# Low part of a block's products by TensorE in some blocks, and list and row products moved to other steps

## The chip, the cores and the metric

The kernel runs on one core of one Trainium2 chip. The metric is the device time of one execution in microseconds (us). Before the change it is 1099.06 us, the median of three runs (1097.8 to 1101.74). Profiles come from one further execution.

The engines are named as in the profile: PE is TensorE (PEld its weight loads), DVE is VectorE, ACT is ScalarE, POOL is GpSimd, and SP issues most of the DMAs.

## The reference

One layer of an edge-gated graph network: 16 graphs of 1024 nodes with 256 features, one sparse weighted adjacency for all of them.

```python
pre_u = jnp.einsum('bud,dk->buk', h_t, W1[:d])
pre_v = jnp.einsum('bvd,dk->bvk', h_t, W1[d:])
hidden = jax.nn.relu(pre_u[:, :, None, :] + pre_v[:, None, :, :] + b1)
S = jax.nn.sigmoid(jnp.einsum('buvk,ko->buvo', hidden, W2)[..., 0] + b2[0])
a_t = jnp.einsum('buv,bud->bvd', S * A_a, h_t)
m_t = jnp.einsum('uv,bud->bvd', A_m, h_t) * h_t
z_t = beta1 * h_t + beta2 * (jnp.einsum('bvd,de->bve', a_t, Wa) + ba) \
    + beta3 * (jnp.einsum('bvd,de->bve', m_t, Wm) + bm)
```

Here `A_a` and `A_m` are both the adjacency. Most of it is zero, so the kernel computes gates only for the edges that are there: it fetches the rows of the neighbours u of a node v.

## The kernel before

**Blocks and steps.** The 16 graphs form 4 groups of 4; the 1024 nodes v form 8 tiles of 128. A block is one group with one tile: 32 blocks, numbered k, in the order of `order` (groups 0 and 1 interleaved in blocks 0 to 15, group 2 in 16 to 23, group 3 in 24 to 31). A block has 10 steps (two windows of 64 nodes, five steps each), so there are 320 steps; n numbers them and s = n mod 10 is the step in its block. In a step 128 edges are handled for the four graphs of the group: the row `fetched` holds, for the edge's node u, four pre-activations and four feature rows.

**One step.** POOL gathers `fetched` (L518) from a table in DRAM, up to 8 steps ahead. PE makes `pc`, the row of pre_v for each edge, as a product of a 0/1 matrix `mark` with `X` (L607, function `expand`, two steps ahead; there are two PSUM buffers named pc). DVE adds `pc` to `fetched` (L639, `add`, one step ahead), and then for each of the four graphs takes relu times W2 with a sum (L647, `gate`). ACT takes the sigmoid (L650) and multiplies the edge's weights with it into `left` (L652). PE sums the neighbours' rows with these weights into `acc` (L664, `aggregate`), two steps' worth in every second step.

**Once in a block.** `halves` makes `X` for the next block, that is pre_v with its bias. The product with `mark` rounds its operands to a shorter format (float32r), so X holds the high part of a value and the low part that the rounding left out: rows 0 to 63 of a window's X are one part of its 64 nodes and rows 64 to 127 the other. In the kernel before, ACT copies the product `p` out twice, as X in the short format (L482) and as `low` in full (L483); DVE subtracts the one from the other (L484); ACT copies both parts to the other half of the rows (L486, L489). Further, a block's end: `half_end` copies `acc` to `ev`, `turn_over` transposes it with `ident` (L682, copied by L685 into `LT`), `block_end` multiplies with Wa and Wm (L713), DVE adds beta1 h (L719) and SP stores.

**Rows and lists.** `rows` makes the table rows of pre_u by PE (L445 with w_u), in two halves with a copy by ACT each (L461), and SP writes them to the table; a row's x and hT are loaded some steps before. `plan` says at which step n each load and each half stands: `loads` and `at`. The products of 8 tiles of groups 0 and 1 are made in the first 51 steps, those of group 2 in steps 68 to 142, those of group 3 in 148 to 222. `lists` makes the lists of neighbours for a tile of nodes: tiles 0 to 3 ahead of the first step, tiles 4 to 7 between the steps, started at the steps of `start_list`. It is a generator: at `yield "op"` it gives way after one DVE operation, at "step" it asks for a later step for its PE work (L289, L341), at "load" and "wait" it pauses for some steps. `piece_of` turns these words into step numbers, and `fill` puts one piece between the operations of `gate`.

**What sets the order.** The order on each engine is written out by hand (a manual schedule): the loop over n issues everything, and each engine executes its own instructions in that order. In step n of the later part the order is: `gather_in` (aggregates and refetches), `add(n + 1)`, `gate(n)`, `left_adj(n + 1)`, `expand(n + 2)`, and then `products(n)`: row products, transposes, block end and the parts of `halves`. `after(step, f)` puts a piece at a later step.

**PSUM.** There are two buffers named `pc` and two named `misc`. The products `p` of `rows` and `halves`, the transposes `pt`, the block end `pz` and the list products `pl` all take turns in the two `misc` buffers, in the order in which they are issued. Who wants a buffer waits until the user before the last has been copied out.

Of the kernel before, what the change touches and what calls it, by code (L numbers as in the profile page):

```python
# [7 lines left out]
FP = mybir.dt.float32  # L8
FR = mybir.dt.float32r
I32 = mybir.dt.int32  # L10
AF = mybir.ActivationFunctionType
# [6 lines left out]
def kernel(  # L18
# [82 lines left out]
    def fixed(shape, name, dt=FP):  # L101
        return const.tile(shape, dt, name=name)
# [70 lines left out]
    slot_of = fixed([P, NW, TW], "slot_of")  # L173
    for w in range(NW):
        nc.vector.tensor_scalar(slot_of[:, w, :], upto[:, :TW], float(P), row, ALU.mult, ALU.add)
    ident = fixed([P, P], "ident")
    nc.vector.tensor_scalar(ident, upto[:, :P], row, None, ALU.is_equal)
    place = upto[:, :W].rearrange("p (q v) -> p q v", v=V)
    slot, nth = upto, upto[:, :S]

# [39 lines left out]
    def small(name):  # L220
        return psm.tile([P, 512], FP, name="misc")
# [20 lines left out]
    def lists(vt):  # L242
# [32 lines left out]
                nc.vector.scalar_tensor_tensor(keys, keys, top[:, s + 7:s + 8], keys, ALU.is_lt, ALU.mult)  # L275
                yield "op"

        used = lst.tile([P, S], FP, name="used", bufs=4)
        nc.vector.tensor_scalar(used, top, 0.0, None, ALU.is_gt, ALU.add, accum_out=R[:, 0:1])
        yield "op"  # L280
        nc.vector.tensor_scalar(R[:, 2:3], row, float(N), float(vt * P * N), ALU.mult, ALU.add)
# [6 lines left out]
        for i in range(4):  # L288
            nc.tensor.matmul(pw[:, i:i + 1], sums[:, i].rearrange("p w q v -> p (w q v)"), R[:, 0:1],  # L289
                             start=True, stop=True)  # L290
        yield "wait"
        first = R[:, 1:2]
        from_ = lst.tile([P, 1], FP, name="from", bufs=4)
# [176 lines left out]

    cuts = {}

    def halves(k):
        X = cuts[k] = big.tile([P, NW, GD], FR, name="X")
        low = one.tile([P, GD], FP, name="low")
        for h in range(2):
            step = yield
            c = slice(2 * h * D, (2 * h + 2) * D)
            p = small("p")
            add_row(p, b1_p)  # L480
            half_product(p, hTs[order[k]], w_v, h, True)
            nc.scalar.copy(X[:, 0, c], p)  # L482
            nc.scalar.copy(low[:, c], p)  # L483
        after(step + (2 if k else 1), lambda: nc.vector.tensor_tensor(low, low, X[:, 0, :].bitcast(FP), ALU.subtract))  # L484
        yield
        nc.scalar.copy(X[W:, 1, :], X[W:, 0, :].bitcast(FP))  # L486
        for w in range(NW):
            yield
            nc.scalar.copy(X[(1 - w) * W:(2 - w) * W, w, :], low[w * W:(w + 1) * W])  # L489
# [133 lines left out]
    def piece_of(r, n):  # L623

        said = next(r[0], None)
        if said is None:
            running.remove(r)
        else:
            r[1:] = said not in ("slot", "step"), n + {"load": 4, "wait": 2, "slot": 1, "step": 1}.get(said, 0)

    def fill(n, gap=True):
        for r in running:
# [3 lines left out]

    def add(n):
        t = fetched[at_slot[n]][:, :GD]
        nc.vector.tensor_tensor(t, t, pcs.pop(n), ALU.add)  # L639

    def gate(n):
        m = len(QUARTERS[n % TW])
# [120 lines left out]


    advance = {0: (3,), 2: (3,), 4: (3,)}
    start_list = dict(zip((0, 16, 48, 88), range(EARLY, NT)))
    loads, at = {}, {}

    def plan(blocks, ns):

        for k, (load, *pieces) in zip(blocks, ns):
            loads[load] = k
            at.update((n, k) for n in pieces)

    plan(turn[NT:], ((0, 1, 8), (1, 9, 12), (9, 18, 19), (13, 22, 28), (20, 29, 32), (29, 38, 39), (33, 42, 48), (40, 49, 51)))
    for g, first in ((2, 60), (3, 140)):
        plan([(g, vt) for vt in range(NT)], ((first - 4 + 10 * i, first + 8 + 10 * i, first + 12 + 10 * i)
                                             for i in range(NT)))
    plan([(1, vt) for vt in range(FIRST)], [(37 + 10 * i,) for i in range(FIRST)])
    plan([(g, vt) for g in range(2) for vt in range(FIRST, NT)], ((103,), (113,), (125,), (133,)))  # L780
# [19 lines left out]
    def products(n, k, s):  # L800
        nonlocal end, parts
        made_rows(n)
        if (s == 2 and 0 < k < BS) or n == total:
            turn_over(k - 1, 1, 1, n)
        z = 3 if n < ROOM else 4
        if z <= s < z + 4 and 0 < k < BS:
            if s == z:
                end = block_end(k - 1)
                next(end)
            go(end, n)  # L810
        if ROOM <= n < total - T:
            if s in (8, 9):
                turn_over(k, 0, s - 8, n)
        elif s == 7 and k < BS:
            turn_over(k, 0, 0, n)
        if s == 7 and k == BS - 1 or s == 8 and n < ROOM:
            turn_over(k, 0, 1, n)
        if (s == 0 and 0 < k < BS) or n == total - 1:
            turn_over(k - (s == 0), 1, 0, n)
        if n == total - 2:  # L820
            end = tail(tails[:2], n)
            next(end)
        elif n == total - 1:
            go(end, n)
        elif n >= total:
            end = tail([tails[2 + n - total]], n)
            next(end)
            go(end, n)
            go(end, n)
        later = n >= ROOM  # L830
        if k + 1 < BS and s - later in (0, 2, 3, 5, 6):
            if s == later:
                parts = halves(k + 1)
                next(parts)
            go(parts, n)

# [22 lines left out]
    done = 0  # L859
    for n in range(total + 2):  # L860
        k, s = divmod(n, T)
        if n < total - 3:
            last_in = n - 1 if n % 2 or n < ROOM else done
        else:
            last_in = n
# [170 lines left out]
```

## Time and profile before

| quantity | value |
|---|---|
| median of 3 runs | 1099.06 us |
| the profiled execution: its own time | 1101.12 us |
| its span, first to last instruction | 1099.3 us |
| busy PE, DVE | 1022.2 us (93%), 1025.4 us (93%) |
| busy ACT, POOL | 872.5 us (79%), 464.3 us (42%) |
| mean granted PE clock | 0.975 |
| DMA, mean over the span | 359 GB/s |

Busy time says how long an engine had an instruction in hand. The matmuls' ends are modelled and matmuls overlap, so a matmul's mean duration is longer than the distance from one to the next. PE and DVE are both busy 93% over the whole span; which of them sets the pace is to be read stage by stage. Blocks can be found in the trace by DVE's additions L639: every tenth begins a block. The first begins at 65.3 us, the last block ends at 1076.1.

### The profile page before, as it was taken

The numbers are of one execution on the slowest core, as the hardware profiler recorded it, in microseconds if no ns is written. First come the engines' busy times: TensorE is split into PE (matmuls) and PEld (weight loads), VectorE is DVE, ScalarE is ACT, GpSimd is POOL, SyncE is SP. The second block draws the span as 40 slices with busy tenths as digits, with TensorE's granted clock in tenths as the row PEclk, the third lists the DMA queues.
The fourth block names the chain that finished last, engine by engine and source line by source line (L and its number), as shares of the span: only waits on it lengthen the run. The fifth ranks groups of instructions, "written<-read, shape, count | busy, mean of one in ns | idle before, by whom it ended". The sixth has DMA issues, their size and how long they took to land.

```text
span 1099.3 us, 23917 instructions
## 1 busy us (share of the span) xinstructions
PE 1022.2 (93%) x7645; PEld 726.5 (66%) x7645; DVE 1025.4 (93%) x3487; ACT 872.5 (79%) x2616; POOL 464.3 (42%) x453
## 2 busy tenths in 40 slices
PE   7777889999899999999999999999999999999986
PEld 6654556776667666676777677767766666666653
DVE  8788888898999999999999999999999999999994
ACT  3347667787778888888988889888889888888873
POOL 2746575445347433563334343433343333333330
PEclk9988989999899999999999999999999999999999
DMA  9999799999999999999999999999999999999991
GB/s 285 331 391 311 295 327 303 356 394 382 384 343 344 391 410 381 384 378 396 408 382 400 406 400 398 386 398 388 353 362 383 372 350 357 359 372 363 354 335 42
DMA packets 149030, 394.54 MB, mean 359 GB/s; under 512 B 18224, under 2 KB 96048, under 8 KB 112688
## 3 DMA queue, kind: packets, MB, share of 16 engines
q0 software_dynamic: 50240, 300.11, 69.6%
q1 hardware_dynamic: 85360, 79.71, 22.9%
q10 hardware_dynamic: 13296, 13.11, 3.6%
q8 instruction: 62, 1.02, 0.3%
q14 instruction: 72, 0.59, 0.1%
HBM read 396.93 MB, written 50.33 MB: 407 GB/s over the span
## 4 chain that ended last, share of the span: by engine, by line
PE 39%; DVE 32%; issue 10%; ACT 9%; DMA 6%; POOL 2%; another core or an unknown queue 0%; SPq 0%; POOLq 0%; DVEq 0%; ACTq 0%
DVE fetched L647 15%; DVE fetched L639 12%; PE acc L664 10%; PE misc L713 10%; PE misc L445 7%; PE pc L607 7%; ACT left L652 3%; PE misc L682 2%; DMA hT<-in_xT_dram 2%; DMA hT<-in_x_dram 2%; PE misc L449 1%; DMA fetched<-table,uidx 1%; DVE low L484 1%; DVE h_blk L719 1%; DVE LT L696 1%
## 5 line engine op out<-in xcount | busy, mean ns | idle before, releaser
L518 POOL DMA_INDIRECT fetched<-table,uidx x320 | 345.5, 1080 | 540.9 <-PE acc L664 384.1
L647 DVE SCALAR_TENSOR_TENSOR fetched<-fetched,w_b 128x256 f32<-128x256 f32 x1280 | 476.5, 418 | 0.0
L639 DVE TENSOR_TENSOR fetched<-fetched,pc 128x1024 f32<-128x1024 f32 x320 | 387.9, 1212 | 38.1 <-PE pc L607 23.1
L652 ACT ACTIVATE left<-left,gt 128x32 f32<-128x32 f32 (+1 forms) x1280 | 299.5, 304 | 10.4
L664 PE MATMUL acc<-fetched,left 128*32 128x256 f32 x4096 | 271.7, 390 | 5.9 <-ACT left L652 4.6
L607 PE MATMUL pc<-X,mark 128*128 128x512 f32 x640 | 245.9, 466 | 12.1 <-DVE fetched L639 12.0
L664 PEld LDWEIGHTS acc<-fetched,left 128*32 128x32 f32 x4096 | 123.7, 111 | 113.1 <-issue 38.8
L650 ACT ACTIVATE gt<-sc,b_b 128x4 f32<-128x4 f32 x320 | 95.5, 298 | 94.8 <-DVE fetched L647 84.4
L607 PEld LDWEIGHTS pc<-X,mark 128*128 128x128 f32 x640 | 106.3, 191 | 91.8 <-issue 48.9
L713 PE MATMUL misc<-w_a,LT 128*128 128x256 f32 x496 | 118.7, 383 | 0.0
L713 PE MATMUL misc<-w_m,LT 128*128 128x256 f32 x496 | 117.2, 379 | 0.0
L445 PE MATMUL misc<-w_v,hT 128*128 128x256 f32 x448 | 108.1, 385 | 1.0 <-DMA hT<-in_xT_dram 1.0
L682 PE MATMUL misc<-ident,ev 128*128 128x128 f32 x512 | 81.3, 282 | 27.0 <-ACT low L483 9.3
L713 PEld LDWEIGHTS misc<-w_a,LT 128*128 128x128 f32 x496 | 94.7, 191 | 15.7 <-issue 0.4
L713 PEld LDWEIGHTS misc<-w_m,LT 128*128 128x128 f32 x496 | 93.9, 189 | 15.2
L617 ACT ACTIVATE left<-onehot,val 128x64 f32<-128x64 bf16 (+1 forms) x320 | 102.9, 322 | 0.0
L385 POOL DMA_INDIRECT val<-in_adjT_dram,vidx x80 | 87.6, 1095 | 33.2 <-issue 18.9
L647 DVE DVE_READ_ACCUMULATOR fetched<-fetched,w_b 128x1 f32 x1280 | 100.4, 78 | 0.0
L682 PEld LDWEIGHTS misc<-ident,ev 128*128 128x128 f32 x512 | 61.2, 143 | 55.1 <-ACT low L483 14.7
L445 PEld LDWEIGHTS misc<-w_v,hT 128*128 128x128 f32 x448 | 86.6, 194 | 16.0 <-DMA hT<-in_xT_dram 1.9
L672 ACT COPY ev<-acc 128x512 f32<-128x512 f32 x128 | 74.7, 584 | 15.4 <-PE acc L664 6.8
L685 ACT COPY LT<-misc 128x512 f32<-128x512 f32 x128 | 73.1, 572 | 5.6 <-PE misc L682 2.9
(178 smaller groups left out, 974.6 us busy)
## 6 DMA issues: line engine op xcount, KB each, us to landing
h_blk<-table SPq DMA_DIRECT2D x62, 256.0 KB
out_dram<-h_blk SPq DMA_DIRECT2D x62, 256.0 KB
hT<-in_xT_dram SPq DMA_DIRECT2D x28, 512.0 KB
table<-in_x_dram ACTq DMA_DIRECT2D x24, 512.0 KB
table<-tab SPq DMA_DIRECT2D x48, 256.0 KB
fetched<-table,uidx POOLq DMA_INDIRECT x320
table<-in_x_dram SPq DMA_DIRECT2D x8, 512.0 KB
table<-fetched SPq DMA_DIRECT2D x8, 512.0 KB
```

The costliest lines, as they stand in the source:

```text
L385: nc.gpsimd.indirect_dma_start(out=val[:, i, j:j + 1], out_offset=None, in_=adj_flat, in_offset=bass.IndirectOffsetOnAxis(ap=vidx[:, i, j: ...
L445: nc.tensor.matmul(p[:, bb * D:(bb + 1) * D], hT[:, 2 * h + bb, i, :], wt[:, i, :], start=(i == 0 and not begun), stop=(i == DC - 1), skip ...
L518: nc.gpsimd.indirect_dma_start(out=fetched[at_slot[n]], out_offset=None, in_=table[g], in_offset=bass.IndirectOffsetOnAxis(ap=uidx[:, vt * ...
L607: nc.tensor.matmul(pcs[n][:, c], marks[n // TW][:, j * P:(j + 1) * P], cuts[k][:, w, c], start=True, stop=True)
L617: nc.scalar.activation(lefts[n][:, :m, 1::GB, :], onehot[:, i, o:o + m, :].unsqueeze(2).to_broadcast([P, m, GB // 2, V]), AF.Copy, scale=v ...
L639: nc.vector.tensor_tensor(t, t, pcs.pop(n), ALU.add)
L647: nc.vector.scalar_tensor_tensor(t[:, b, :], t[:, b, :], 0.0, w2_b, ALU.max, ALU.mult, accum_out=sc[:, b:b + 1])
L650: nc.scalar.activation(gt, sc, AF.Sigmoid, bias=b2_b)
L652: nc.scalar.activation(lefts[n][:, :m, 2 * b, :], lefts[n][:, :m, 1 + b // 2 * GB, :], AF.Copy, scale=gt[:, b:b + 1])
L664: nc.tensor.matmul(accs[h][b * 2 * V:(b + 1) * 2 * V, r, :], left[:, i, 2 * b - b % 2:2 * b - b % 2 + 2].rearrange("p k v -> p (k v)"), f[ ...
L682: nc.tensor.transpose(pt[:, r, :, c, :], ev[:, r, c * P:(c + 1) * P], ident)
L713: nc.tensor.matmul(pz[:, bb * D:(bb + 1) * D], LTs[k][:, 2 * h + bb, i if bb else 1 - i, c, :], wt[:, c, :], start=False, stop=(i == 0 and ...
```

## The change

**Low part by PE.** For blocks k with `turned(k)`, that is 2 to 11 and 24 to 31, a new function `halves_turned` makes X. ACT writes X with its sign turned, -round(p). A step or two later PE adds the product of the identity (`ident_r`, now in the short format; `ident` is the same bits) with X onto p in its PSUM buffer, so that p - round(p), the low part, stands there; ACT copies it, again with the sign turned, straight into the two places. The tile `low` and the subtraction by DVE fall away for these blocks. `pc` comes out with its sign turned, so `add` subtracts for them. The parts stand at the ends of steps 1 and 3, and at the heads of steps 3 and 5. Each half's `p` now keeps its misc buffer from the first part to the second.

**Row products.** `plan` gets other steps: in the early blocks the halves stand in steps 7 to 0 of a block, and the loads come up to 9 steps earlier. For group 2, halves that stood at step 2 of a block stand at step 0 up to block 10. Blocks from 11 on are unchanged.

**Lists.** The pieces after a "step" are put off to steps 7 to 0 of a block, the first list's load gets 7 steps instead of 4, the lists start at steps 0, 14, 44 and 72 instead of 0, 16, 48 and 88, and from list 3 on ACT copies the four columns of `pw` out of PSUM at once, so that DVE reads the copy. `used` has one buffer less.

```diff
-    ident = fixed([P, P], "ident")
-    nc.vector.tensor_scalar(ident, upto[:, :P], row, None, ALU.is_equal)
+    ident_r = fixed([P, P], "ident_r", FR)
+    nc.vector.tensor_scalar(ident_r, upto[:, :P], row, None, ALU.is_equal)
+    ident = ident_r.bitcast(FP)
...
-        used = lst.tile([P, S], FP, name="used", bufs=4)
+        used = lst.tile([P, S], FP, name="used", bufs=3)
...
+        if vt >= EARLY - 1:
+            pw_ = lst.tile([P, 4], FP, name="pw", bufs=1)
+            nc.scalar.copy(pw_, pw[:, :4])
+            pw = pw_
         yield "wait"
...
+    def turned(k):
+        return 2 <= k <= 11 or k >= 24
+
+    def halves_turned(k):
+        X = cuts[k] = big.tile([P, NW, GD], FR, name="X")
+        for h in range(2):
+            yield
+            c = slice(2 * h * D, (2 * h + 2) * D)
+            p = small("p")
+            add_row(p, b1_p)
+            half_product(p, hTs[order[k]], w_v, h, True)
+            nc.scalar.activation(X[:, 0, c], p, AF.Copy, scale=-1.0)
+            nc.scalar.copy(X[W:, 1, c], X[W:, 0, c].bitcast(FP))
+            yield
+            nc.tensor.matmul(p, ident_r, X[:, 0, c], start=False, stop=True, skip_group_check=True)
+            for w in range(NW):
+                nc.scalar.activation(X[(1 - w) * W:(2 - w) * W, w, c], p[w * W:(w + 1) * W], AF.Copy, scale=-1.0)
...
-            r[1:] = said not in ("slot", "step"), n + {"load": 4, "wait": 2, "slot": 1, "step": 1}.get(said, 0)
+            n += {"load": 4 if n else 7, "wait": 2, "slot": 1, "step": 1}.get(said, 0)
+            while said == "step" and n > ROOM and 0 < n % T < 7:
+                n += 1
+            r[1:] = said not in ("slot", "step"), n
...
-        nc.vector.tensor_tensor(t, t, pcs.pop(n), ALU.add)
+        nc.vector.tensor_tensor(t, t, pcs.pop(n), ALU.subtract if turned(n // T) else ALU.add)
...
-    start_list = dict(zip((0, 16, 48, 88), range(EARLY, NT)))
+    start_list = dict(zip((0, 14, 44, 72), range(EARLY, NT)))
...
-    plan(turn[NT:], ((0, 1, 8), (1, 9, 12), (9, 18, 19), (13, 22, 28), (20, 29, 32), (29, 38, 39), (33, 42, 48), (40, 49, 51)))
+    plan(turn[NT:], ((0, 1, 8), (1, 9, 10), (9, 17, 18), (11, 19, 20), (19, 27, 28), (21, 29, 30), (29, 38, 39), (31, 40, 48)))
     for g, first in ((2, 60), (3, 140)):
-        plan([(g, vt) for vt in range(NT)], ((first - 4 + 10 * i, first + 8 + 10 * i, first + 12 + 10 * i)
+        plan([(g, vt) for vt in range(NT)], ((first - 4 + 10 * i, first + 8 + 10 * i, first + (10 if first + 10 * i < 100 else 12) + 10 * i)
                                              for i in range(NT)))
...
-        if k + 1 < BS and s - later in (0, 2, 3, 5, 6):
+        if k + 1 < BS and s - later in ((0, 2) if turned(k + 1) else (0, 2, 3, 5, 6)):
             if s == later:
-                parts = halves(k + 1)
+                parts = (halves_turned if turned(k + 1) else halves)(k + 1)
                 next(parts)
             go(parts, n)
...
         k, s = divmod(n, T)
+        if s in (3, 5) and turned(k + 1) and k + 1 < BS:
+            go(parts, n)
```

## The prediction

> **What bounds the kernel now.** I read the span first by stage, cut at the starts of the blocks (the first addition of every tenth step): block 0 is 65.3 to 101.4 us, blocks 1 to 6 end at 323.4, 7 to 10 at 453.1, block 11 at 483.3, 12 to 22 at 819.5, 23 to 30 at 1050.4. The windows view gives, for each, length, busy us of PE, PEld, DVE, ACT and POOL, the granted clock, the DMA share and GB/s:
>
> ```profile
> 65.30:101.40 36.10, 28.56 (x157) 18.11 (x158) 30.83 (x107) 21.44 (x65) 19.04 (x21) 0.82 0.96 363
> 101.40:323.40 222.00, 204.50 (x1456) 145.59 (x1455) 202.15 (x710) 166.67 (x498) 116.98 (x115) 0.94 0.95 346
> 323.40:453.10 129.70, 123.33 (x955) 88.47 (x958) 125.82 (x432) 108.15 (x328) 59.35 (x56) 1.00 1.01 378
> 483.30:819.50 336.20, 329.49 (x2567) 238.10 (x2569) 321.12 (x1050) 295.71 (x892) 125.22 (x113) 1.00 1.01 390
> 819.50:1050.40 230.90, 222.52 (x1755) 152.70 (x1748) 230.90 (x762) 205.95 (x633) 82.57 (x81) 1.00 0.96 363
> ```
>
> Four regimes. In blocks 23 to 30 DVE never idles: 230.9 / 8 = 28.86 us a block, all DVE. In 12 to 22 (336.2 / 11 = 30.56) PE leads with 98% and DVE idles 1.4 us a block. In 7 to 10 both idle some. In 1 to 6 (37.0 a block) each idles about 20 us in all, and the clock is 0.94. The chain of waits (start, us, engine and line) confirms it: first three lines of the last group, then of the middle, then of the early part.
>
> ```profile
> 923.60 1.16 DVE fetched L647 x7
> 925.02 1.14 DVE low L484
> 926.16 1.13 DVE fetched L639
> ...
> 807.90 1.86 PE acc L664 x32
> 809.76 0.66 PE pc L607 x2
> 810.42 1.73 PE misc L713 x8
> ...
> 115.74 3.42 PE misc L445 x8
> 150.43 0.23 PE misc L449
> 73.44 10.65 DMA key<-in_adjT_dram
> ```
>
> The subtraction L484 is on the path in the last group and costs 1.14 us there (its row says 1.25; it overlaps its neighbours). Then the waits: of PE in blocks 12 to 22 (first line), of PE before 323.4 (next three), of DVE there (last).
>
> ```profile
> PE misc L682 <- ACT low L483: 5.7, 9, 0.7
> ...
> PE misc L445 <- ACT low L483: 3.8, 2, 3.1
> PE misc L682 <- ACT LT L685: 3.5, 3, 1.5
> PE misc L682 <- issue: 3.3, 1, 3.3
> ...
> DVE key L252 <- DMA key<-in_adjT_dram: 3.2, 1, 3.2
> ```
>
> The PE lines are one thing: the two PSUM buffers named misc. A product waits until ACT has copied out an earlier one. Last, the prices, from the rows by form (busy, mean ns):
>
> ```profile
> L484 DVE TENSOR_TENSOR low<-low,X 128x1024 f32<-128x1024 f32 x32 | 40.0, 1248 | 0.0
> L489 ACT CAST X<-low 64x1024 fp32r<-64x1024 f32 x64 | 66.9, 1045 | 1.2
> L483 ACT COPY low<-misc 128x512 f32<-128x512 f32 x64 | 37.3, 583 | 0.0
> L449 PE MATMUL misc<-b_p,unit 128*128 128x512 f32 x64 | 26.8, 419 | 2.0 <-issue 1.3 <-ACT left L617 0.7
> ```
>
> **What the Trainium skill says.** "TensorE: Matmul & The Clock Gate", Back-to-back issue gap: 512 columns, warm, follow each other after 216 ns although one alone takes longer; the chain agrees (L449 0.23 us in it, 419 ns in its row). So a matmul's row overstates what it adds. The same page, Part 1: after an idle window of about 3.4 us the clock falls to half. The trace agrees: the L445 group at 115.74 takes 3.42 us after a PE gap of 3.1, elsewhere 1.73. "ScalarE: Activation LUTs", What ACT_TABLE_LOAD costs: with immediate scale an ACTIVATE takes 186 ns + 0.833 ns an element, an estimate of 0.61 us for 512; copies of 512 take 0.57 to 0.58 here. "Perfetto Trace Analysis", Roofline: one core's 16 DMA engines end near 435 GB/s; the middle moves 390, the last group 363.
>
> **The last group (halves of blocks 24 to 31, made in 23 to 30).** Removed: one L484, 1.14 us of DVE a block, 27.72 left. The subtraction in place of the addition costs the same. ACT: before 2 x 0.57 + 2 x 0.58 + 1.04 + 2 x 1.05 = 5.4 us; after 2 x 0.57 and six half-height pieces of 512, 2 x 0.57 + 6 x 0.6 = 4.7; ACT was idle 3.1 of 28.9 us, so this hides. Added on PE: two matmuls with ident_r, like L449 (same 128x128 weights, same 512 columns): 0.23 us each by the chain, 0.42 by the row. I take 0.47 a block, since they stand in a dense row of matmuls. PE by chain prices: ten L607 pairs of about 0.62, 64 aggregate matmuls at 1.86 per x32 (7.4), four L713 groups and two L445 groups of 1.73, four L449 of 0.23, four L682 groups of 0.46: 26.8, with the change 27.3. The middle blocks calibrate this: with two more L445 groups the same sum is 30.2, and the block takes 30.56, 0.36 above the larger engine. So the new block is 27.72 + 0.3 = 28.0, 0.85 saved, eight times, less 0.3 for the first block, which starts with PE late: **-6.5**. From above: 8 x 1.14 = 9.1. From below: by the modelled PE idle, (230.9 - 222.5) / 8 = 1.05, and 2 x 0.42, only 0.2 is left to gain: 1.7. What is late next is PE's order at steps 3 and 5, where the ident matmul stands first and waits for ACT's X copy, with the aggregates, the next product pair and so DVE's addition behind it. That copy is issued two steps (5 us) earlier, so I price the wait at 0; if ACT were late it would cost its lateness there. ACT in turn now waits at those heads for PE, with ev, mark and gate copies queued behind; aggregates use their gates a step later, which covers it. DMA: 363 GB/s x 28.86 / 28.0 = 374, below the 390 of the middle, where DVE waited only 0.3 us on a gather: nothing.
>
> **Blocks 7 to 10.** Removed 4 x 1.14 from DVE: 125.8 to 121.2. PE 123.3 + 4 x 0.47 = 125.2, so PE leads here; at 0.36 a block over it 126.6 against 129.7: **-3**. The idle of PE that must go for this is the misc wait of L682 (0.7 to 1.5 us a block at step 3), and it does go: no row product stands at step 2 in these blocks any more. If PE's idle (6.4) stayed, 131.6: +2. If all PE work went for its chain price, -5.
>
> **Blocks 1 to 6.** DVE loses 6 x 1.14 = 6.8 and gets 3.2 us of list 4 (eight L261 of 0.29 and four small ones) that stood in block 0. PE gets 6 x 0.47 = 2.8; the row products are 14 before and after. The misc waits above are 10.6 us of PE; behind two of them, of over 3 us each, PE runs at half rate (1.7 us lost on the L445 group, about 2.8 after the other). Not all of this reaches DVE, which idles 20 us for several reasons; I count 8. The five copies of pw (128x4, about 0.2 us on ACT) free a buffer sooner. Against that, the row products of blocks 1 to 3 now stand in steps 7 to 0 in a bunch: in the built order PE's steps 7, 8, 9, 0 and the next 1 hold (chain prices) 3.5, 4.9, 4.7, 2.8 and 4.2, 20.1 us, where DVE has about 16 with list work; two pc buffers let PE be ahead by one step, 2.8, so DVE stalls some 1 to 3 us a block, 3 to 9 in three blocks. Net -3.6 - 8 + 9, about **-3**; ends -14 (no stalls from the bunch, clock full) and +8 (old stalls stay too).
>
> **Block 0.** The first list's load gets 7 steps instead of 4, so the 3.2 us wait of DVE on key, which is on the chain, should go; The DMAs stay the same in number. SP issues hT loads up to 9 steps earlier; each waits for an hT_ buffer that row products free, and behind it on SP stand output stores and h_blk loads with several steps to spare. The copies of x into the table, issued on ACT at 0.56 us each, and POOL's whose and val transfers move with the loads and lists; POOL is busy 42% and mostly waits for free slots. I count nothing for these. PE is at clock 0.82 there and may be late next: **-2.5**, ends -6 and 0. Blocks 11 to 22, 31 and the end are untouched.
>
> **Sum.** -6.5 - 3 - 3 - 2.5 = -15. The profiled execution took 1101.1 (span 1099.3 and 1.8 around it), 0.2% over the median of the three runs, 1099.06; taken off the median: **1084**.
>
> **The rivals.**
> 1. PE takes over everywhere: the ident matmuls cost their row (0.42), the last group gains 2, blocks 1 to 10 nothing, block 0 2.5: 1094.5. For it: PE at 97% of the last group as modelled. Against: the chain has hardly any PE there, and two more L445 groups cost the middle only 1.7.
> 2. The other side, slower: the bunch of row and list products in steps 7 to 0 starves DVE. Place: PE's queue ahead of the pc product, blocks 1 to 6. Price: 2 to 4 us a block, with steps of 4 to 5 us against DVE's 2.8. It decides once it passes the 12 us gained elsewhere; with +2 a block left over, the early part costs +12, blocks 7 to 10 +2, against -6.5 and nothing in block 0: about 1106. For it: four row groups in succession, 6.9 us. Against: DVE has list work in the same steps, and before had steps of 5.7.
> 3. The early part loses all its stalls: -14 and -5 there, with -6.5 and -2.5: 1071.
> That the change doesn't do what it says is excluded: the built order has two ident_r matmuls a block and no L484 in those blocks.
>
> **Numbers.** Forecast 0.52 (1076 to 1092), rival 1 0.18, rival 2 0.18, rival 3 0.12. Least change that a measurement of this kernel can tell is about 0.3%, 3.3 us. Faster: forecast, rival 3, and half of rival 1, 0.73; same 0.09; slower 0.18. The range runs from 1073 to 1100, with most of rival 2 and half of rival 3 outside.
>
> **What would show it.** In the changed profile: blocks 23 to 30 at about 28.0 us with DVE idle a few tenths; no L682 waiting on a copy of low before 453; PE clock of blocks 1 to 6 near 0.97; no 3.2 us wait of DVE on key. Wrong would be: last blocks at 28.6 or more with PE busy throughout (ident matmuls dearer than 0.23), or DVE waits on pc of over 10 us gathered at steps 8 to 1 of blocks 1 to 3.

## The result and the profile after

| | before | changed |
|---|---|---|
| median of four runs each, same session | 1099.38 us | 1116.32 us |
| ratio, 95% interval | | 1.0152 [1.0133, 1.0172] |
| profiled execution, its span | 1101.12, 1099.3 | 1116.06, 1114.2 |
| busy PE, DVE | 93%, 93% | 93%, 90% |
| share of the chain of waits: PE, DVE | 39%, 32% | 55%, 23% |

The change made the kernel slower, by 1.5% in this comparison. Two more comparisons of the same two programs, in later sessions, gave 1.0009 and 1.0027: the changed kernel was in none of them faster, and how much slower it is differs between them; the experiments come back to this. All ratios here leave out runs of over 1.5% above the fastest of the same kernel, so they can differ a little from the quotient of the medians. DVE lost work (1025.4 to 1006.8 us busy), and the time it was freed of went into waiting for PE.

The windows view of the changed kernel, cut at the same block starts as before (length, busy us of PE, PEld, DVE, ACT, POOL, clock, DMA share, GB/s): block 0, blocks 1 to 6, 7 to 10, 11, 12 to 22, 23 to 30.

```profile
65.90:100.00 34.10, 27.12 (x162) 17.34 (x163) 28.78 (x97) 19.76 (x61) 17.64 (x19) 0.90 0.97 372
100.00:323.40 223.40, 205.99 (x1455) 146.58 (x1452) 196.44 (x710) 164.74 (x511) 115.55 (x115) 0.95 0.96 341
323.40:454.70 131.30, 126.64 (x958) 90.31 (x958) 123.15 (x437) 106.80 (x332) 63.29 (x64) 1.00 1.02 378
454.70:489.10 34.40, 31.41 (x232) 21.97 (x231) 29.38 (x97) 26.00 (x80) 16.29 (x15) 0.95 0.99 356
489.10:825.50 336.40, 329.27 (x2568) 238.62 (x2570) 321.07 (x1050) 296.11 (x892) 125.28 (x111) 1.00 1.01 390
825.50:1064.60 239.10, 223.78 (x1750) 155.72 (x1744) 223.50 (x754) 203.06 (x644) 81.11 (x80) 0.97 0.94 347
```

Against before, stage by stage: block 0 -2.0, blocks 1 to 6 +1.4, 7 to 10 +1.6, block 11 +4.2 (30.2 to 34.4), 12 to 22 +0.2, 23 to 30 +8.2; with +0.6 ahead of the first addition and +0.7 behind the last, that is the span's +14.9. The last group is the large one. Its DVE did lose what it should (230.9 to 223.5 us busy, 0.93 a block), but each block now holds about 1.95 us in which DVE waits; before it held none. Of the 8 blocks four took 29.26 us and four 30.51, two and two in turn, against 28.86 before.

What DVE and PE wait for there, from the waits view of blocks 23 to 30 (who waits, for whom: us in all, times, longest):

```profile
PE misc L492 <- ACT X L489: 15.0, 8, 1.9
DVE fetched L665 <- PE acc L690: 11.2, 6, 2.1
```

L492 is the ident matmul, L489 ACT's copy of X ahead of it. Once in each block PE stands 1.9 us before that matmul, and the aggregates, the next pair of expand matmuls and then DVE's addition come late behind it. The timeline of one such place, steps 1 to 3 of block 24 (start, us, engine, line, operation, operands; in brackets idle time before it and who ended it):

```profile
860.16 1.89 PE L450 MATMUL misc<-w_v,hT__6859 128*128 128x256 f32 x8
...
862.18 0.73 ACT L573 CAST mark<-whose 128x640 fp32r<-128x640 uint8 x1
862.27 0.08 DVE L673 DVE_READ_ACCUMULATOR fetched<-fetched,w_b 128x1 f32 x1
...
862.35 0.64 PE L708 MATMUL misc<-ident_r,ev 128*128 128x128 f32 x4
...
862.81 0.30 ACT L676 ACTIVATE gt<-sc,b_b 128x4 f32<-128x4 f32 x1
...
863.14 0.96 ACT L678 ACTIVATE left<-left,gt 128x32 f32<-128x32 f32 x4
864.00 0.41 DVE L673 SCALAR_TENSOR_TENSOR fetched<-fetched,w_b 128x256 f32<-128x256 f32 x1
864.01 0.33 ACT L640 ACTIVATE left<-onehot,val 128x64 f32<-128x64 bf16 x1
864.25 0.57 ACT L489 ACTIVATE X<-misc 128x512 fp32r<-128x512 f32 x1
...
864.87 0.50 PE L492 MATMUL misc<-X,ident_r 128*128 128x512 f32 x1 [1.88 <-ACT X L489]
...
865.30 1.50 PE L690 MATMUL acc<-fetched,left 128*32 128x256 f32 x24
```

The product p is finished at 862.05 (860.16 + 1.89; a modelled end). ACT does not start on it for another 2.2 us: in ACT's own order its copy stands behind the copy of `mark` (L573), the step's sigmoid (L676), the four `left` multiplications (L678) and a piece for the next step (L640). The gate that the sigmoid needs is done at 862.35, but ACT reaches it only at 862.81, and it has no pause of more than 0.03 us in this stretch. So what makes the copy late here is ACT's own queue, and it is so in all eight blocks. From the end of p to the ident matmul it is 2.82 us. PE has between them only step 2, an expand pair and four transposes (L708), done at 862.99, 0.94 us later, and then idles 1.88 us.

The chain of waits of the changed kernel, a little later in the same block, has PE where it had DVE (compare the first three lines of the chain in the prediction):

```profile
868.04 1.73 PE misc L450 x8
869.77 0.46 PE pc L630 x2
870.22 0.23 PE misc L454
870.46 1.73 PE misc L739 x8
872.18 0.23 PE misc L492
872.41 1.91 PE acc L690 x32
```

The ident matmul of step 5 (872.18) does not wait, and takes 0.23 us in the chain, as priced. Only the one at step 3 waits.

The difference between blocks of 29.26 and 30.51 us is the clock. The windows view again, at two places of one 1.88 us stop each; the last three numbers of a line are clock, DMA share and GB/s:

```profile
861.34:864.75 3.41, 1.65 (x10) 1.08 (x8) 3.41 (x13) 3.38 (x10) 0.30 (x1) 1.00 1.02 427
864.75:868.16 3.41, 3.21 (x30) 1.71 (x31) 3.41 (x16) 3.28 (x11) 1.61 (x2) 1.00 1.02 417
...
892.06:895.47 3.41, 1.53 (x23) 0.76 (x25) 3.41 (x11) 3.28 (x12) 0.00 (x0) 1.00 1.01 425
895.47:898.89 3.42, 3.42 (x18) 2.15 (x11) 3.42 (x11) 3.35 (x12) 1.98 (x2) 0.50 0.96 372
```

The clock changes only at points 3.41 us apart. In the first pair the stop (862.99 to 864.87) crosses such a point, and at most 1.76 us of it lie in one window: the clock stays 1.00. In the second pair PE is busy 1.53 of 3.41 us, so 1.88 us of idling lie in one window, and the next one runs at 0.50. That window costs the block 30.51 - 29.26 = 1.25 us.

Of the prices by form, over the whole run of the changed kernel (busy us, mean ns, idle before):

```profile
L494 ACT ACTIVATE X<-misc 64x512 fp32r<-64x512 f32 x72 | 42.6, 592 | 1.1
L489 ACT ACTIVATE X<-misc 128x512 fp32r<-128x512 f32 x36 | 21.2, 588 | 8.5 <-PE misc L450 5.4 <-PE pc L630 2.8
L492 PE MATMUL misc<-X,ident_r 128*128 128x512 f32 x36 | 20.0, 556 | 23.7 <-ACT X L489 23.7
```

ACT's pieces cost what was estimated (0.6). What was not is the 23.7 us of PE idle time before L492: 15.0 in the last group, and the rest in the early blocks.

### The profile page after: what moved, and what is told of

The parts are those of the page before. It is cut to its first block, busy times and chain, and to the rows that moved or that the text cites. A ratio compares the mean times of both kernels' runs of the same rounds, so it can differ in the third digit from the quotient of the medians.

```text
span 1114.2 us, 23979 instructions
## 1 busy us (share of the span) xinstructions
PE 1031.7 (93%) x7681; PEld 735.3 (66%) x7681; DVE 1006.8 (90%) x3469; ACT 864.2 (78%) x2639; POOL 460.8 (41%) x453
## 4 chain that ended last, share of the span: by engine, by line
PE 55%; DVE 23%; ACT 12%; issue 7%; another core or an unknown queue 1%; DMA 1%; DVEq 0%; ACTq 0%
PE acc L690 14%; PE misc L739 13%; PE misc L450 12%; DVE fetched L673 12%; PE pc L630 9%; DVE fetched L665 7%; ACT left L678 4%; PE misc L708 2%; PE misc L454 2%; ACT mark L573 1%; ACT gt L676 1%; ACT LT L711 1%; ACT left L640 1%; ACT ev L698 1%; PE misc L492 1%
## 5 line engine op out<-in xcount | busy, mean ns | idle before, releaser
L678 ACT ACTIVATE left<-left,gt 128x32 f32<-128x32 f32 (+1 forms) x1280 | 299.5, 304 | 10.4
L690 PE MATMUL acc<-fetched,left 128*32 128x256 f32 x4096 | 268.0, 392 | 3.0 <-issue 1.6
L676 ACT ACTIVATE gt<-sc,b_b 128x4 f32<-128x4 f32 x320 | 95.2, 298 | 79.4 <-DVE fetched L673 68.1
L450 PE MATMUL misc<-w_v,hT 128*128 128x256 f32 x448 | 110.3, 391 | 0.0
L640 ACT ACTIVATE left<-onehot,val 128x64 f32<-128x64 bf16 (+1 forms) x320 | 102.9, 322 | 0.0
L450 PEld LDWEIGHTS misc<-w_v,hT 128*128 128x128 f32 x448 | 88.8, 198 | 14.8
L708 PE MATMUL misc<-ident_r,ev 128*128 128x128 f32 x512 | 78.9, 277 | 16.7 <-ACT low L506 9.4
L708 PEld LDWEIGHTS misc<-ident_r,ev 128*128 128x128 f32 x512 | 61.5, 141 | 40.3 <-ACT low L506 14.2
```

Source lines behind the costliest of these rows:

```text
L450: nc.tensor.matmul(p[:, bb * D:(bb + 1) * D], hT[:, 2 * h + bb, i, :], wt[:, i, :], start=(i == 0 and not begun), stop=(i == DC - 1), skip ...
L640: nc.scalar.activation(lefts[n][:, :m, 1::GB, :], onehot[:, i, o:o + m, :].unsqueeze(2).to_broadcast([P, m, GB // 2, V]), AF.Copy, scale=v ...
L676: nc.scalar.activation(gt, sc, AF.Sigmoid, bias=b2_b)
L678: nc.scalar.activation(lefts[n][:, :m, 2 * b, :], lefts[n][:, :m, 1 + b // 2 * GB, :], AF.Copy, scale=gt[:, b:b + 1])
L690: nc.tensor.matmul(accs[h][b * 2 * V:(b + 1) * 2 * V, r, :], left[:, i, 2 * b - b % 2:2 * b - b % 2 + 2].rearrange("p k v -> p (k v)"), f[ ...
L708: nc.tensor.transpose(pt[:, r, :, c, :], ev[:, r, c * P:(c + 1) * P], ident)
```

## The experiments

My theory after the result: the last group loses 8 us through the round trip PE - ACT - PE at step 3 and the clock behind it, while the moves of rows and lists gain. Against it stood three rivals: the two extra matmuls themselves are dear (rival 1 of the prediction); the moves cost the time (rival 2); and the ident matmul is only put a little too early, so that a place behind the aggregates repairs it. All ratios are to the kernel before, run beside it on the same chip; its median was 1104 to 1106 us in these sessions, so only ratios are compared between them.

**The last group alone.** `e1_last_only`: rows and lists as before, and

```diff
     def turned(k):
-        return 2 <= k <= 11 or k >= 24
+        return k >= 24
```

> Only blocks 24 to 31 get the turned low part; rows and lists stand as in the kernel before. Theory 1 (the ident matmul at the head of step 3 waits 1.9 us for ACT's copy of X): the last group takes 239 us as in the changed kernel instead of 231, everything ahead of it as before; time before +8, about 1107. Rival (the last group is slow because it inherits a late state from the changed early part): last group near 231 or below, 1093 to 1099.

1112.59 us, ratio 1.0087 [1.0062, 1.0112]. In its profile blocks 23 to 30 take 239.2 us at clock 0.97, as in the changed kernel; the other stages are within 1 us of those of the kernel before in e11 (below). The last group's loss needs nothing from the early part.

**The ident matmul a little later.** `e2_last_later`: as e1, with the matmul behind the step's aggregates.

```diff
-        if s in (3, 5) and turned(k + 1) and k + 1 < BS:
-            go(parts, n)
...
             gather_in(done)
             done += 1
+        if s in (3, 5) and turned(k + 1) and k + 1 < BS:
+            go(parts, n)
```

> As e1, but the ident matmul and the two copies after it stand behind the step's aggregates instead of ahead of them, which gives ACT 1.4 us more. Theory 1: PE's wait for the copy of X falls from 1.9 us to about 0.5, the half-rate windows go, and the last group takes 28.1 to 28.5 us a block, 225 to 228; time about 1094 to 1097. Rival (two more matmuls are simply too much for PE, whatever they wait for): the last group stays at 236 or more, time 1104 or more.

1108.24 us, ratio 1.0042 [1.0010, 1.0075]. The windows view of its blocks 23 to 30, and a line of its waits there:

```profile
822.40:1057.30 234.90, 223.36 (x1752) 154.39 (x1748) 222.82 (x753) 202.81 (x643) 83.26 (x80) 1.00 0.95 356
```

```profile
PE misc L450 <- ACT LT L705: 11.5, 8, 1.5
```

About half of the loss is gone (239.2 to 234.9), and the clock is full again; no stop is longer than 1.5 us. But a new wait of 1.4 us a block stands at the product of the second half (its bias matmul, L450 of this kernel): the first p holds one of the two misc buffers until the ident matmul is done and copied out, so this product must take the buffer of the transposes, which ACT's LT copy frees late. A held buffer is passed over, so the turns are not strict here: in the changed kernel the second half's product begins at 867.54, while ACT copies from the first p until 868.71. The place was too early, and that is not all of it.

**More room by another step.** `e8_last_step0`: all moves, turned in blocks 24 to 31 alone, and there the first half's product one step earlier, with its ident matmul at the end of step 2; the second half's product stays at the end of step 3 and its ident matmul at the head of step 5.

```diff
-        if s in (3, 5) and turned(k + 1) and k + 1 < BS:
+        if s == 5 and turned(k + 1) and k + 1 < BS:
...
+        if turned(k + 1):
+            later = 0
-        if k + 1 < BS and s - later in ((0, 2) if turned(k + 1) else (0, 2, 3, 5, 6)):
+        if k + 1 < BS and s - later in ((0, 2, 3) if turned(k + 1) else (0, 2, 3, 5, 6)):
```

> Both moves, and the turned low part for blocks 24 to 31 with other places: first product at the end of step 0, its ident matmul at the end of step 2, second product at the end of step 3, its ident matmul at the head of step 5 as before. Theory 1 (what costs is that PE wants a result of ACT within a step or so, while ACT is about a step behind PE; the two matmuls themselves cost 0.25 us each): PE waits for copies of X fall under 0.3 us, the last group takes 27.8 to 28.3 us a block, 223 to 227, and the time is 5 below e4, about 1087. Rival (PE cannot take the two matmuls): last group 232 or more.

1102.42 us, ratio 1.0000 [0.9973, 1.0028], that is some 12 us behind the moves alone. Its last group takes 240.6 us, though no ident matmul waits for X. The wait went to the buffers instead:

```profile
PE misc L454 <- ACT LT L711: 18.6, 16, 1.3
```

Twice a block a product now waits for a misc buffer. Giving the round trip more time and giving the buffer back early pull against each other while there are two buffers. Two other ways were not tried: a third misc buffer, and ACT's copy of p ahead of the copy of `mark` and the gate's pieces in ACT's order.

**The matmuls without the round trip.** `e9_no_sub_two_matmuls`: the kernel before; in the last group DVE's subtraction is left out and PE does two more matmuls of the same shape that wait for nobody.

```diff
             p = small("p")
+            if k >= 24:
+                add_row(p, b1_p)
             add_row(p, b1_p)
...
-        after(step + (2 if k else 1), lambda: nc.vector.tensor_tensor(low, low, X[:, 0, :].bitcast(FP), ALU.subtract))
+        if k < 24:
+            after(step + (2 if k else 1), lambda: nc.vector.tensor_tensor(low, low, X[:, 0, :].bitcast(FP), ALU.subtract))
```

> The kernel before, but for blocks 24 to 31 the subtraction on DVE is left out (X then carries the whole product in the place of its low part), and PE gets two more matmuls a block of the size of the ident ones, that wait for nothing new and whose result the next matmul overwrites. Theory 1 (the matmuls cost 0.25 us each; the round trip from PE over ACT to PE and the held misc buffer cost the rest): the last group takes 27.7 to 28.1 us a block, 222 to 225. Rival (PE cannot take them): 230 or more.

1098.43 us, ratio 0.9937 [0.9893, 0.9980]. Its blocks 23 to 30 in the windows view:

```profile
822.40:1045.60 223.20, 219.42 (x1760) 154.94 (x1756) 222.32 (x754) 203.47 (x633) 84.71 (x80) 1.00 0.99 375
```

27.90 us a block, DVE-bound again (222.32 of 223.20), clock full. Same arithmetic on PE and DVE as in the changed last group, 16.0 us less time than e1: this difference is the round trip over ACT, with the held buffer and the clock that come with it, 2.0 us a block. The matmuls are as cheap as the forecast took them.

**Is it X that must be waited for?** `e10_no_wait_for_x`: as e1, with a constant in place of X as the matmul's operand.

```diff
-            nc.tensor.matmul(p, ident_r, X[:, 0, c], start=False, stop=True, skip_group_check=True)
+            nc.tensor.matmul(p, ident_r, b1_p.unsqueeze(1).to_broadcast([P, 2, D]), start=False, stop=True, skip_group_check=True)
```

> As e1, but the ident matmul adds the bias rows in place of X, so that it needs nothing of ACT (the low part is left out of the result); it keeps its place, and p keeps its misc buffer as long. Theory 1: the wait of 1.9 us before it goes; a wait of the second product at step 3 for the misc buffer comes in its place, about 1.4 us as in e2, so the last group stays between 232 and 236. Rival (the wait for X alone is the cost): 224 to 227.

1114.22 us, ratio 1.0103 [1.0016, 1.0191], and the same wait line as the changed kernel's:

```profile
PE misc L488 <- ACT X L485: 15.0, 8, 1.9
```

The experiment did not separate what it was meant to, but it shows something else: the matmul adds onto p, and ACT must have read p before it may. With constants for its other operands, p is all that still ties it to ACT. So another operand, or a second copy of X, takes nothing away; the wait lies in the idea of adding onto a tile that another engine still has to read.

**The subtraction on POOL instead.** `e13_pool_sub`: rows as before, lists moved, nothing turned; in the last group POOL subtracts, a step earlier.

```diff
-        after(step + (2 if k else 1), lambda: nc.vector.tensor_tensor(low, low, X[:, 0, :].bitcast(FP), ALU.subtract))
+        after(step + (2 if 0 < k < 24 else 1), lambda: (nc.gpsimd if k >= 24 else nc.vector).tensor_tensor(low, low, X[:, 0, :].bitcast(FP), ALU.subtract))
```

> The moved lists of e7, no turned low part; for blocks 24 to 31 the subtraction of X from low is issued to POOL, one step earlier, instead of DVE. Theory 1 (nothing but the work on DVE bounds the last group, and no round trip through PE is added): the last group at 223 to 226, as in e9, the time 6 to 7 under e15. Rival (POOL takes over 2 us for it, keeps the next gathers or ACT's copies waiting, or slows DVE beside it): last group at 230 or more.

1106.78 us, ratio 1.0019 [0.9991, 1.0046]; the lists alone, run beside it (e15, below), gave 0.9911, so this lost 11 us. Blocks 23 to 30 take 241.3 us. Its timeline shows why:

```profile
889.86 0.41 DVE L673 SCALAR_TENSOR_TENSOR fetched<-fetched,w_b 128x256 f32<-128x256 f32 x1
890.15 2.37 POOL L507 TENSOR_TENSOR low<-low,X 128x1024 f32<-128x1024 f32 x1 [4.04 <-ACT low L506]
890.21 0.07 DVE L673 DVE_READ_ACCUMULATOR fetched<-fetched,w_b 128x1 f32 x1
890.21 2.60 DVE L673 SCALAR_TENSOR_TENSOR fetched<-fetched,w_b 128x256 f32<-128x256 f32 x1
```

A gate operation that takes 0.41 us took 2.60 beside POOL's 2.37 us subtraction: DVE stood still for nearly all of it. The Trainium skill, "SBUF — State Buffer", section "SBUF: two separate sides", says this: POOL and DVE share a pair of memory ports, held for a whole instruction, and a DVE instruction with two inputs in SBUF is shut out meanwhile. The measurement agrees: the last group's 320 gate operations average 472 ns here and 414 before, 320 x 58 ns or 8 x 2.3 us in all, where DVE's own subtraction would have cost 8 x 1.14.

**The early part.** `e3_early_only` turns blocks 2 to 11 alone (`return 2 <= k <= 11`) with all moves; `e4_moves_only` turns none (`return False`); `e6_rows_only` keeps of the moves only the row products, with the lists as before; `e7_lists_only` only the lists, with the row products as before.

```diff
     def turned(k):
-        return 2 <= k <= 11 or k >= 24
+        return 2 <= k <= 11
```

and in e4, e6 and e7 `return False`; in e6, against the changed kernel, also

```diff
-            n += {"load": 4 if n else 7, "wait": 2, "slot": 1, "step": 1}.get(said, 0)
-            while said == "step" and n > ROOM and 0 < n % T < 7:
-                n += 1
+            n += {"load": 4, "wait": 2, "slot": 1, "step": 1}.get(said, 0)
...
-    start_list = dict(zip((0, 14, 44, 72), range(EARLY, NT)))
+    start_list = dict(zip((0, 16, 48, 88), range(EARLY, NT)))
```

and no copy of `pw`; in e7 also

```diff
-    plan(turn[NT:], ((0, 1, 8), (1, 9, 10), (9, 17, 18), (11, 19, 20), (19, 27, 28), (21, 29, 30), (29, 38, 39), (31, 40, 48)))
+    plan(turn[NT:], ((0, 1, 8), (1, 9, 12), (9, 18, 19), (13, 22, 28), (20, 29, 32), (29, 38, 39), (33, 42, 48), (40, 49, 51)))
...
-first + (10 if first + 10 * i < 100 else 12) + 10 * i
+first + 12 + 10 * i
```

> Turned low part in blocks 2 to 11 alone, with the moved rows and lists; blocks 24 to 31 as before. Theory 1: the last group is back at 231, so 8 less than the changed kernel, about 1108; blocks 0 to 11 as in the changed kernel, 6 longer than before. Rival (late state inherited): last group above 231.

> No turned low part at all, only the moved rows and lists. Theory 2 (the row and list products in a bunch in steps 7 to 0 starve DVE in blocks 1 to 3, about 11 us of waits, and the lighter DVE pays part of it back): blocks 0 to 11 longer than in e3, by up to 10 x 1.1 us; time 1108 to 1118. Rival (the early ident matmuls and their waits cost, the moves are harmless): blocks 0 to 11 at or below before, time 1093 to 1100.

> No turned low part; of the moves only the row products (lists as before, pw read in PSUM). Theory 3 (the gain of e4 is the missing wait for list 4's key, in block 0, and so the lists' part): no gain, 1099 to 1104, block 0 at 36 to 38. Rival (the gain comes from row products that no longer meet the halves in the misc buffers): 1092 to 1096 with blocks 1 to 6 near 216.

> No turned low part; of the moves only the lists (row products as before). Theory 3: block 0 at 31 and the time 1092 to 1096. Rival: block 0 at 31, but blocks 1 to 6 take the 5 us back, 1098 to 1103.

> The moved lists alone once more (the kernel of e7): ratio to before again 0.985 to 0.991; blocks 23 to 30 at 231.

| | turned early | rows moved | lists moved | median us | ratio, 95% interval |
|---|---|---|---|---|---|
| e3 | yes | yes | yes | 1092.50 | 0.9910 [0.9878, 0.9943] |
| e4 | no | yes | yes | 1091.86 | 0.9893 [0.9867, 0.9918] |
| e6 | no | yes | no | 1100.37 | 0.9956 [0.9929, 0.9984] |
| e7 | no | no | yes | 1091.76 | 0.9878 [0.9850, 0.9906] |
| e15, the kernel of e7 once more | no | no | yes | 1095.71 | 0.9911 [0.9887, 0.9934] |

Three things follow. The turned halves of blocks 2 to 11 bring nothing that can be measured (e3 against e4). The moves bring 1.1%, and the lists alone bring all of it; row products moved by themselves gain 0.4%, but add nothing to the lists that can be measured. In e6's profile block 0 takes 38.4 us, as theory 3 had it, and blocks 1 to 6 take 216.0, as its rival had it. And rival 2's bunch is not there: in e4, blocks 1 to 6 take 216.1 us, and the DVE waits in them are

```profile
DVE h_blk L745 <- ACT LT L744: 9.7, 2, 5.7
DVE fetched L665 <- PE pc L630: 2.9, 4, 1.6
```

so 2.9 us on pc, where the bunch was to cost 3 to 9. With the halves turned (e3) the second line reads

```profile
DVE fetched L665 <- PE pc L630: 13.8, 12, 3.2
```

DVE's saved time is given back as waits for PE, and PE's own longest waits there are at the ident matmul, 7.1 us in three.

**One number of the lists.** `e12_load7`: the kernel before with only the first list's load given 7 steps.

```diff
-{"load": 4, "wait": 2, "slot": 1, "step": 1}
+{"load": 4 if n else 7, "wait": 2, "slot": 1, "step": 1}
```

> The kernel before with one number changed: the first list's load gets 7 steps instead of 4. Theory 3 (the gain of the moved lists is mostly the wait of DVE for list 4's key in block 0): block 0 at 32 to 34 and 3 to 5 less than before, about half of what e7 gains. Rival: nothing, since the list's work then only comes later.

1094.14 us over four runs, ratio 0.9896 [0.9828, 0.9964]. Beside it `e11_before_again`, the kernel before, took 1107.60 (its ratio to the other runs of the same kernel 1.0012 [0.9983, 1.0042]).

> The kernel before, for its stages on this chip. Theory (blocks 12 to 30 take the same time in every execution, blocks 0 to 11 vary from one to the next): blocks 12 to 22 at 336 and 23 to 30 at 231 within 1, blocks 0 to 11 anywhere from 410 to 430.

e11's profile has, in its block 0 of 38.6 us, the wait that this edit is about:

```profile
DVE key L252 <- DMA key<-in_adjT_dram: 5.1, 1, 5.1
```

In e12 the wait is gone and block 0 takes 31.1 us. Of these 7.5 us, 5.1 are the wait; another 2.2 are list work of DVE (31.0 to 28.8 us busy) that is no gain, since it now stands behind block 0 (201.5 to 204.2 us busy in blocks 1 to 6). Expected were 3 to 5 us. The ratio says 12, with an interval from 4 to 19, and the two profiled executions differ by 2.9. So the constant gains, and perhaps as much as all the moves together; intervals of this width do not tell, and of the gain only the wait of 3 to 5 us has a shown cause.

The other stages of e11 came out as expected: 416.9 us in blocks 0 to 11, 336.0 in 12 to 22 and 230.9 in 23 to 30. But the theory does not hold for blocks 12 to 22: with the same program there, e6's profile has 340.8 us, and e15's, of its slowest execution, 347.6.

**The changed kernel again.** `e5_again` and `e14_changed_third` are the changed kernel unaltered.

> The changed kernel once more, beside runs of the same chip. Theory 1 and 2 with parts that add up: early part as in e3 and last group 8 longer: about 10 more than e3, 1100. Rival (its first 11 blocks are slow on their own, by stalls that fall at other places in each build): again 1110 to 1117, with the surplus in blocks 0 to 11.

> The changed kernel a third time. Theory (the surplus of the first comparison in blocks 0 to 11 is a place where stalls happened to fall, not the change): last group 239, ratio to before between 0.995 and 1.006. Rival (the change really costs 1.5%): ratio 1.013 or more, with blocks 0 to 11 above those of before.

1104.92 us, ratio 1.0009 [0.9982, 1.0037], and 1105.94, ratio 1.0027 [1.0000, 1.0054]. Within the intervals that is what the parts add up to: about -11 from the moves, +8 to +10 from the last group (e1), nothing from the early turning. Neither interval overlaps that of the first comparison. The stages of e5 in the windows view (block 0, blocks 1 to 6, block 11) show where the first run was worse:

```profile
64.90:96.00 31.10, 26.49 (x158) 17.34 (x158) 28.78 (x94) 20.31 (x63) 15.62 (x18) 0.88 1.00 388
96.00:313.20 217.20, 199.60 (x1459) 144.16 (x1457) 195.56 (x712) 164.57 (x510) 118.54 (x119) 0.98 0.98 356
443.70:474.20 30.50, 29.92 (x233) 21.73 (x232) 29.06 (x96) 26.16 (x80) 15.44 (x15) 1.00 1.01 387
```

34.1 against 31.1, 223.4 against 217.2 at clock 0.95 against 0.98, 34.4 against 30.5 at 0.95 against 1.00; the last group is the same (239.1 and 239.2). The profile of the first comparison has its further 14 us wholly in blocks 0 to 11: 423.2 us, against 409.2 in e5 and 409.6 in e14. PE idles more there (32.1 against 27.2 us in e5), and the clock is 0.96 against 0.98. That profile is of one of four executions, all at 1116 to 1117 us; what put them there, and not the later ones, was not found.

**The better version.** Of what was run, the lists moved and nothing else changed (e7, e15) is faster than both kernels, by 0.9 to 1.2% against before. By their intervals e3, e4 and e12 can't be told from it.

## Why the prediction was wrong

**The last group** was forecast at -6.5 and came out at +8.2. The failed step, as the prediction put it: "That copy is issued two steps (5 us) earlier, so I price the wait at 0; if ACT were late it would cost its lateness there." The copy is issued at the end of step 1 and wanted at the head of step 3, so one step lies between, in which PE is done 0.94 us behind p; and ACT has 2.2 us of other work queued ahead of the copy. The wait is 1.9 us a block, and in four of the eight blocks a window of 3.41 us at half clock follows. That ACT "was idle 3.1 of 28.9 us" is a mean over the block; at this place ACT has no slack. That it was called the next thing late was right; counting it in steps, and not in PE's work between the two points of its order, gave 5 us for what is about 1. Another cost has no term in the prediction, p's longer hold of a misc buffer. It did not decide in the changed kernel, whose PE waits in the last group at the ident matmul alone, but it is the reason why moving the matmul (e2, e8) repairs only half or none. The rest of this step held: 27.90 us a block with neither wait (e9) against the forecast 28.0, so the matmul's price of 0.23 and DVE's saving were right. Rival 1, its matmuls dearer, is refuted by e9: PE does become the bound, but by standing still.

**Blocks 7 to 10**, forecast -3: +1.6 here, and 130.5 and 130.6 us in e5 and e14, against 129.7. This is close to the end "If PE's idle (6.4) stayed, 131.6: +2". PE's waits at the transposes did go, from 4.8 to 0.5 us, and 1.8 us at the ident matmul came; PE idles 4.7 us. But PE's busy time rose by 3.3 us, where 1.9 were priced. A difference of this size can't be ascribed to the change from one profile each: e4 and e8, which run the same program there, with nothing turned, take 131.2 and 127.8.

**Blocks 1 to 6**, forecast -3: +1.4 in the first comparison, 217.2 us in e5 and e14 against 222.0 and, in e11, 218.6 before. So -1 to -5, as forecast, but by other terms: e4 reaches 216.1 with nothing turned, e6 216.0 with the rows alone moved, and the bunch's 9 us were nearly all absent.

**Block 0**, forecast -2.5: -2.0 here, but 31.1 us in e5 against 36.1 and, in e11, 38.6 before, so -5 to -7.5. The mechanism was right, the size too small. The wait for the list's load is 3.2 us in one run and 5.1 in another, and about 2 us of list work of DVE (30.8 to 28.8 us busy) moved out of the block. The prediction put this work on blocks 1 to 6, as 3.2 us, but did not take it off block 0.

**The rivals.** Rival 2 said slower, through the moved products in the early blocks; slower it was, but the moves gained and the turned halves of the last group lost. Rival 3 did not come either: the clock of blocks 1 to 6 is 0.95 and, in e5, 0.98, so stops remain. The 14 us in blocks 0 to 11 of the first comparison belong to no term of the prediction, and no run explained them.

## What to carry to other kernels

When work of a busy engine is replaced by a chain over two others, price the chain by what the waiting engine has to do between its two ends in its own order, not by the number of steps between; here 0.94 us of PE's work stood against a round trip of 2.82. Read in the trace what the engine in the middle has queued ahead of the new piece; its mean idle time over a block is no slack at that place. A matmul that adds onto a tile that another engine still has to read holds both the engine and the buffer: with two buffers, of the two other places tried one won back half of the loss and one nothing. And before a large rearrangement, look for the single late load: one constant gave here 0.4 to 1.7%, the rearrangement 0.8 to 1.3%.

## What was not expected of the hardware

- **Less than an idle window can suffice.** The Trainium skill, "TensorE: Matmul & The Clock Gate", Part 1, gives a free-running window of 3413 ns and half clock "after ≥1 idle window (~3.4µs)". The window agrees (3.41 us). The condition does not; the prediction counted half clock only behind stops of over 3 us. In the last group of the changed kernel 1.86 to 1.88 us of idling in one window was followed by one window at 0.50 (four blocks), 1.57 to 1.76 us was not (the other four). But this is no threshold. Here are two windows, each with the next one, the first pair from the changed kernel and the second from the kernel before. They show half clock behind 1.64 and 1.27 us of idling:

```profile
134.30:137.71 3.41, 1.77 (x10) 1.56 (x11) 3.41 (x12) 1.98 (x8) 2.68 (x3) 1.00 0.96 361
137.71:141.13 3.42, 3.42 (x10) 2.70 (x9) 0.72 (x6) 0.59 (x1) 2.81 (x3) 0.50 0.87 239
...
286.83:290.24 3.41, 2.14 (x16) 1.71 (x14) 3.41 (x11) 3.07 (x10) 1.23 (x1) 1.00 1.04 419
290.24:293.65 3.41, 1.87 (x13) 1.11 (x16) 3.41 (x11) 2.74 (x13) 0.00 (x0) 0.50 1.02 417
```

  In e1, a window with 1.89 us of idling (from 113.60) was followed by full clock. What decides is open.
- **POOL's subtraction stops DVE's two-input operation altogether** (2.60 us in place of 0.41), so it costs DVE 2.2 us where its own subtraction costs 1.14.
- **Some transfers come very late, and at the same places.** With the row products as before, ACT waits in block 4 or 5 for one write of table rows: 5.1 to 12.7 us in nine of ten profiles (12.7 in e2, 9.8 in e9 and in e12); the first profile of the kernel before has no such wait. With them moved no wait of this kind is over 4.3 us, which may be what e6 gains. For an hT load in block 13 PE waits 10.5 us in e15, 9.8 in e7 and 4.6 in e14; in e15 one that was issued at 495.0 landed at 521.9. The profiles of e7 and e15 are of the slowest execution of each. Why these transfers are late was not found. Stages of one profile apiece can differ by that much, and so the verdicts on the early part rest on the repeated times.
